# Swin attention and a Fourier layer on one core: the division of the first sixteen rows is split between GpSimd and ScalarE, and the mode scalings change shape and place

## The chip, the cores and the metric

The kernel runs on one core of one Trainium2 chip. The metric is the device time of one execution in microseconds, lower is better. A core has TensorE (PE; its weight loads are listed as PEld), VectorE (DVE), ScalarE (ACT), GpSimd (POOL) and SyncE (SP), which issues nearly all DMAs here. Each engine works through its own list of instructions in order; between engines, semaphores order the work. All data is float32.

## The reference

The input x is 32 images of 56x56 pixels with 128 channels. Two residual layers follow one another, each on a group norm (32 groups of 4 channels, statistics over a whole image).

```python
x = x + L0(_gn(x))     # shifted window attention: 7x7 windows, shift 3, 4 heads of 32 channels
x = x + L1(_gn(x))     # Fourier layer with a feed-forward behind it

# L0, for each window of 49 tokens
qkv  = win @ w_qkv.T                          # q scaled by 32 ** -0.5
attn = softmax(q @ k.T + bias + mask)         # 49 x 49 for each head
out  = (attn @ v) @ w_proj.T + b_proj         # written back unshifted

# L1, once along the width and once along the height
f   = dct(x)[..., :32]                        # 32 modes
g   = einsum(f, w)                            # one 128 x 128 matrix per mode
y   = idct(g, padded with zeros)              # both directions are added
out = relu(y @ W1 + b1) @ W2 + b2             # 512 hidden channels
```

## The kernel before

**Rows and cycles.** An image is cut into 8 rows of 8 windows (NWR = 8), so there are 256 window rows. The program is one loop over cycles, and cycle r starts row r. The stages of a row are spread over cycles: queries, keys, scores, maximum, exponential and v in cycle r (`attn_qk`, `attn_scores`, `attn_max`, `attn_exp`, `attn_v`), the division by the row sums in cycle r+1 (`attn_recip`, `attn_divide`), a transpose in cycle r+2 (`attn_transpose`), the product with v and the projection in cycle r+3 (`attn_values`, `attn_project`), the sums for the second group norm in cycle r+4 (`attn_sums`, `attn_squares`). In between, the input of the next image is turned, its statistics are taken and its first norm is worked out (`norm_step`).

The Fourier layer of image b begins in cycle 8b + 11 (CONV_BEGIN is 11). With c counted from there: c = 0 computes the statistics and the width transform, c = 1 and 2 the two halves of the height transform, c = 3 to 5 mix the modes, c = 5 to 8 transform back, and c = 8, 9, 10, 12, 13, 14, 15 run the seven groups of the feed-forward. These run beside the attention rows of the next two images.

**The order.** The lists of PE, ACT, DVE and POOL are written out by hand: cycles 0 to 10 by `first_rows`, later ones by the calls `halves_first`, `eighths`, `quarters`, `attn_max`, `last_fetch`, `columns_turn`, `behind_max`, `load_first` and `halves_last` of the main loop. Only SyncE's DMAs are placed by a scheduler. Every tile comes from a pool with a tag and a number of buffers (`bufs`); a new tile of a tag waits until the oldest one of the tag has been read for the last time.

**Softmax of a row.** The scores stand in a buffer `a` of 128 partitions x 16 x 49: two windows of 49 rows side by side (partitions 0 to 48 and 64 to 112), 16 groups of 49 columns. VectorE adds bias and mask while it reads PSUM (L486) and takes the maximum (L496), GpSimd subtracts it (L497), ScalarE takes the exponential (L503), VectorE sums (L508) and takes the reciprocal `rs` (L510). Then GpSimd multiplies by `rs` (L522), and at the same time cuts the 49 columns into a block of 32 and one of 17 and moves blocks between groups of 32 partitions, so that one VectorE transpose in blocks of 32x32 (L532) turns all of it. That takes six instructions a row: one of 512 elements and one of 272 on 128 partitions, and two of each on 32 partitions. The result `blocks` has two buffers, taken in turn. There are three buffers `a` for rows 0 to 8 and two later.

**PSUM.** The attention uses four banks in turn (`attn_bank`, tag pa), the rest another four (`conv_bank`, tag pc). A cycle takes a pair for q and k, a pair `po` for the product with v, a pair for the scores, then one for v (`attn_v`) and one for the projection. So v gets the bank that the first of `po` had. Of `po`, u = 0 is read by ScalarE (L579) and u = 1 by VectorE (L577), both into `oT`.

**The statistics and modes.** `fourier_stats` is a generator, and each `next` runs it up to the next `yield`. It averages on TensorE (L650), takes the group sums `ms` (L663), then -mean^2 (L665) and variance + eps (L669) on VectorE, the power -1/2 on GpSimd (L673), and after the first `yield` the shift (L677) on VectorE. The width transform gives four PSUM tiles in c = 0, each half of the height transform two. `turn_modes` transposes each on VectorE into a tile of 448 elements (L715; tag z, four buffers, which also serves the copies of the mixing), and `scale_modes` multiplies it by `rstd` on ScalarE into `y` (L722). There, the 56 lines of one mode lie side by side. `shift_modes` (L727) adds the shift to mode 0. The mixing (L747) reads `y`. In ScalarE's list, the width scalings stand behind v and ahead of exp, the height scalings and both shifts behind exp. `load_columns` (L734, tag htok, two buffers) loads x by columns from DRAM for the height transform: two tiles in c = 0, two in c = 1.

Of the kernel before, what the change touches and what calls it, by code (L numbers as in the profile page):

```python
# [9 lines left out]
F32 = mybir.dt.float32  # L10
AF = mybir.ActivationFunctionType
ALU = mybir.AluOpType
AX = mybir.AxisListType

P = 128
# [32 lines left out]
def swin_fourier_kernel(  # L48
# [33 lines left out]
    def attn_bank():  # L82
        return bank("pa", 4)
# [215 lines left out]
    def attn_buffer(r):  # L299
        return a_sb[r % 3 if r < CONV_BEGIN - 2 else r % 2]  # L300
# [204 lines left out]
    def attn_recip(r):  # L505
# [4 lines left out]
        nc.vector.reciprocal(rs, sm)  # L510
        return rs

    def attn_divide(r, rs):
        a3 = attn_buffer(r).rearrange("p t w j -> p (t w) j")
        dst = blocks[r % 2]
        lo, hi = (slice(0, KB), slice(KB, JP)), (slice(JP, JP + KB), slice(JP + KB, P))
        halves = [(slice(0, P), slice(0, P), k, k) for k in range(2)]
        for a, b in (lo, hi):
            halves += [(a, b, 1, 0), (b, a, 0, 1)]
        for to, src, k, kb in halves:  # L520
            n = (KB, WT - KB)[kb]
            nc.gpsimd.tensor_tensor(  # L522
                dst[to, k, :, :n],
                a3[src, :, kb * KB : kb * KB + n],
                rs[src].unsqueeze(2).to_broadcast([src.stop - src.start, 2 * NWR, n]),
                ALU.mult,
            )
# [7 lines left out]
    def attn_values(im, i, r):  # L535


        v = v_sb[r % 3]
        po = [attn_bank(), attn_bank()]
        HALF = RT // 2  # L540
        po4 = [p[:, :HALF].rearrange("p (r n s) -> p n r s", r=WS, s=WS) for p in po]
        eT = im.eT.pop(i)
# [101 lines left out]
    def fourier_stats(im):  # L644
        pg = attn_bank()

        for k, t in enumerate((im.tot, im.part[:, (NWR - 1) % 4])):
# [13 lines left out]
        )  # L661
        ms = small.tile([P, 2], F32, tag="ms", name="ms")
        nc.vector.tensor_reduce(ms, own, axis=AX.X, op=ALU.add)  # L663
        nm2 = small.tile([P, 1], F32, tag="nm2", name="nm2")
        nc.vector.scalar_tensor_tensor(  # L665
            out=nm2, in0=ms[:, 0:1], scalar=-1.0, in1=ms[:, 0:1], op0=ALU.mult, op1=ALU.mult
        )
        ve = small.tile([P, 1], F32, tag="ve1", name="ve1")
        nc.vector.scalar_tensor_tensor(  # L669
            out=ve, in0=nm2, scalar=1e-5, in1=ms[:, 1:2], op0=ALU.add, op1=ALU.add  # L670
        )
        rstd = small.tile([P, 1], F32, tag="rstd1", name="rstd1")
        nc.gpsimd.tensor_tensor(rstd, ve, mhalf, ALU.pow)  # L673
        im.rstd = rstd
# [33 lines left out]

    def turn_modes(im, width, h):

        im.modes[width, h] = []
        for p in im.py.pop((width, h)):
            t = work.tile([P, 4, C], F32, tag="z", name="modes", bufs=4)
            t = t.rearrange("p k c -> p (k c)")[:, : 2 * CH * KB]
            nc.vector.transpose(t, p[:, : 2 * CH * KB])  # L715
            im.modes[width, h].append(t)

    def scale_modes(im, width, h):

        y = y_of[width][:, : NM * S].rearrange("p (k h n r) -> p h r n k", k=NM, h=2, r=2)[:, h]  # L720
        for r, t in enumerate(im.modes.pop((width, h))):
            nc.scalar.mul(y[:, r], t.rearrange("p (n k) -> p n k", k=NM), im.rstd)  # L722

    def shift_modes(im, width):

# [204 lines left out]
    def divide(cycle):  # L930
        if row(cycle - 1)[0]:
            attn_divide(cycle - 1, attn_recip(cycle - 1))

    def turn(cycle):
        im, i = row(cycle - 2)
        if im:
            attn_transpose(im, i, cycle - 2)
# [54 lines left out]
    def half_columns(cycle, rest=False):  # L992
        for im, c in fourier(cycle):
            if rest and c != 3:
                continue
            if c == 0:
                next(im.stats, None)
            elif c == 3:
                for g in range(2):
                    mix(im, False, g + 2 * rest)  # L1000
            elif c in (4, 5):
                for g in (2 * c - 8, 2 * c - 7):
                    mix(im, True, g)
# [17 lines left out]
    def eighths(cycle):  # L1021
        im, i = row(cycle - 3)
        if im:
            attn_values(im, i, cycle - 3)
        for im, c in fourier(cycle):
            if c == 0:
                for h in range(2):
                    transform(im, True, h)
                    turn_modes(im, True, h)
            if c in (1, 2):  # L1030
                transform(im, False, c - 1)
                if c == 1:
                    for g in range(2):
                        load_columns(im, g + 2)
# [10 lines left out]

    def first_scale(cycle):
        for im, c in fourier(cycle):
            if c == 0:
                shift_modes(im, True)
            elif c in (1, 2):  # L1050
                scale_modes(im, False, c - 1)
                if c == 2:
                    shift_modes(im, False)

    def width_scale(cycle):
        for im, c in fourier(cycle):
# [43 lines left out]
    def halves_last(cycle):  # L1100
        im, i = row(cycle)
        if im:
            attn_v(im, i, cycle)
        width_scale(cycle)
        if has_ff(cycle):
            half_columns(cycle)
        half_columns(cycle, True)
# [3 lines left out]
            norm_step(cycle)  # L1111
        if row(cycle)[0]:
            attn_exp(cycle)
        first_scale(cycle)
        im, j = row(cycle - 3)
        if im:
            last_out(cycle)
# [11 lines left out]
    def first_rows(cycle):  # L1129
# [23 lines left out]
        next_tokens(cycle)  # L1153
        if im:
            attn_v(im, i, cycle)
        if cycle == 0:
            for half in range(2):
                bias_and_mask(nc.vector, 1, 1, half)
# [20 lines left out]
    with tc.manual_schedule(engines={ET.PE, ET.Activation, ET.DVE, ET.Pool}):  # L1179
# [15 lines left out]
        for cycle in range(NB * NWR + CONV_BEGIN + FF_AT[-1] - NWR + 1):  # L1195
# [4 lines left out]
            if not row(cycle - 3)[0]:  # L1200
# [4 lines left out]
                half_columns(cycle)  # L1205
                half_columns(cycle, True)
                first_scale(cycle)
                load_first(cycle)
                last_out(cycle)
                quarters(cycle)  # L1210
# [76 lines left out]
```

## Time and profile before

| | us |
|---|---|
| three runs: median (lowest to highest) | 3299.6 (3297.3 to 3299.78) |
| the profiled execution | 3297.98 |
| its span, first to last instruction | 3296.2 |

| engine | busy us | share of the span | instructions |
|---|---|---|---|
| PE | 3170.4 | 96% | 65408 |
| PEld | 2394.9 | 73% | 65408 |
| DVE | 2605.2 | 79% | 5098 |
| ACT | 2057.4 | 62% | 3680 |
| POOL | 2335.7 | 71% | 2610 |

| line, engine, what | count | mean ns |
|---|---|---|
| L497 POOL subtract the maximum, 128x784 | 253 | 1508 |
| L522 POOL divide, 128x512 / 128x272 | 253 / 253 | 1061 / 660 |
| L522 POOL divide, 32x512 / 32x272 | 506 / 506 | 1054 / 655 |
| L503 ACT exp, 128x784 | 253 | 859 |
| L722 ACT scale modes, 128x448 | 256 | 1122 |
| L715 DVE transpose modes, 128x448 | 256 | 619 |
| L755 ACT copy of the mixing, 128x512 | 256 | 589 |
| L809 ACT copy xf, 128x448 | 192 | 594 |
| L351 ACT copy of wrapped rows, 128x168 | 31 | 337 |
| L629 ACT square, 128x512 / 128x384 | 128 / 128 | 719 / 617 |
| L532 DVE transpose of blocks, 128x1024 | 256 | 1225 |

The profile is one execution, recorded by the hardware; L numbers are lines of the kernel before. Three kinds of its answers are used below. A timeline line gives start and duration in us, engine, line, operation, tile written and tiles read, shapes and count, and in brackets how long the engine had been idle and what released it; a few instructions of one group are merged into one line, with the time from the first start to the last end. A line of waits gives the waiting instruction, its releaser, the total in us, the number of times, and the longest. In a table by stage, each row is one stretch of the run with the busy time of each engine and the number of instructions, then the granted TensorE clock, the share of DMA time and GB/s. Because engine times overlap, shares say little about what a saving is worth: that depends on which wait ends last at the place in question.

### The profile page before, as it was taken

Reading aid. Unit: us, or ns where it says so; the run is one execution under the profiler, and the core shown is the slowest. Engines: PE = TensorE matmul, PEld = TensorE weight load, DVE = VectorE, ACT = ScalarE, POOL = GpSimd, SP = SyncE. Lnnn points to the kernel's source line nnn. Section 1 sums busy time; section 2 is a strip of 40 time slices with the busy share of each in tenths; the row PEclk is TensorE's granted clock in tenths of the full one; section 3 lists DMA queues with packets and bytes.
Section 4 is the critical chain, followed back from the end, with each engine's and each line's share of the span. In section 5 each row is a group of like instructions: output and inputs, shape, how many; then the busy total and the mean of one; then the engine's idle time right before and its main releaser. Section 6 shows DMA issues by size and latency. Waiting matters only on the chain.

```text
span 3296.2 us, 151336 instructions
## 1 busy us (share of the span) xinstructions
PE 3170.4 (96%) x65408; PEld 2394.9 (73%) x65408; DVE 2605.2 (79%) x5098; ACT 2057.4 (62%) x3680; POOL 2335.7 (71%) x2610
## 2 busy tenths in 40 slices
PE   4689999999999999999999999999999999999999
PEld 3467777777777777777777777777777777777776
DVE  7888888887888878888888888877888887888751
ACT  3456666666666666666666666666666666666663
POOL 7777777777777777777777777777777777777741
PEclk9799999999999999999999999999999999999999
DMA  6555555555555555555555555555555655555453
GB/s 105 116 124 142 140 138 142 133 146 140 137 140 135 136 145 138 138 142 138 139 144 143 136 142 138 136 142 143 137 139 136 143 139 139 138 143 135 121 140 96
DMA packets 1168160, 448.40 MB, mean 136 GB/s; under 512 B 520107, under 2 KB 1137629, under 8 KB 1167493
## 3 DMA queue, kind: packets, MB, share of 16 engines
q1 hardware_dynamic: 1159300, 437.38, 54.9%
q8 instruction: 514, 8.42, 1.1%
q10 hardware_dynamic: 7584, 1.18, 0.3%
q14 instruction: 154, 1.25, 0.1%
q0 software_dynamic: 608, 0.17, 0.0%
HBM read 276.97 MB, written 161.48 MB: 133 GB/s over the span
## 4 chain that ended last, share of the span: by engine, by line
PE 76%; ACT 10%; DVE 7%; POOL 3%; DMA 2%; issue 2%; SPq 1%; ACTq 0%; POOLq 0%; DVEq 0%
PE pc L113 35%; PE pa L113 9%; PE pa L456 7%; PE pc L747 5%; PE pc L786 5%; PE pa L592 5%; PE pa L478 4%; PE pa L547 4%; ACT k L443 2%; PE pc L699 2%; ACT hid L830 2%; ACT y L722 2%; POOL a L497 2%; DVE modes L715 1%; DVE a L486 1%
## 5 line engine op out<-in xcount | busy, mean ns | idle before, releaser
L522 POOL TENSOR_TENSOR blocks<-a,rs 128x512 f32<-128x512 f32 x1518 | 1289.4, 856 | 483.9 <-DVE rs L510 263.0
L113 PE MATMUL pc<-wff,hid 128*64 128x128 f32 x12544 | 742.0, 273 | 1.3 <-ACT hid L830 1.0
L113 PE MATMUL pc<-xf,wff 128*64 128x512 f32 (+2 forms) x3584 | 718.9, 539 | 1.1 <-DVE xf L804 0.9
L113 PEld LDWEIGHTS pc<-wff,hid 128*64 128x64 f32 x12544 | 706.5, 137 | 11.1 <-ACT hid L830 5.3
L497 POOL TENSOR_TENSOR a<-a,mx 128x784 f32<-128x784 f32 x253 | 381.4, 1508 | 314.9 <-DVE mx L496 281.6
L113 PEld LDWEIGHTS pc<-xf,wff 128*64 128x64 f32 x3584 | 280.6, 136 | 354.9 <-issue 239.9
L830 ACT ACTIVATE hid<-pc,b1sb 128x512 f32<-128x512 f32 (+2 forms) x896 | 499.4, 643 | 42.7 <-PE pc L113 42.7
L463 ACT COPY v<-pa 128x512 f32<-128x512 f32 x256 | 151.9, 593 | 482.8 <-PE pa L456 482.7
L113 PE MATMUL pa<-xw,wn 128*64 128x392 f32 x2048 | 400.4, 501 | 31.3 <-ACT wn L412 28.8
L865 DVE TENSOR_TENSOR res<-pc,res 128x512 f32<-128x512 f32 (+3 forms) x257 | 142.9, 567 | 319.4 <-issue 173.2
L503 ACT ACTIVATE a<-a 128x784 f32<-128x784 f32 x253 | 217.3, 859 | 281.4 <-POOL a L497 281.4
L486 DVE TENSOR_TENSOR a<-pa,bm 128x392 f32<-128x392 f32 x506 | 261.1, 557 | 84.8 <-PE pa L478 70.6
L837 POOL TENSOR_TENSOR res<-res,b2sb 128x512 f32<-128x512 f32 (+2 forms) x256 | 265.3, 1042 | 87.4 <-DMA res<-scr 78.4
L443 ACT ACTIVATE k<-pa,bqkv,heads 128x392 f32<-128x392 f32 x512 | 318.1, 673 | 8.0 <-PE pa L113 0.9
L532 DVE STREAM_TRANSPOSE eT<-blocks 128x1024 f32<-128x1024 f32 x256 | 313.6, 1225 | 2.4 <-POOL blocks L522 2.4
L127 POOL TENSOR_TENSOR xr<-xr,bproj 128x384 f32<-128x384 f32 (+1 forms) x256 | 292.8, 1144 | 25.6 <-DMA xr<-in_x_dram 17.1
L456 PE MATMUL pa<-wn,xw 128*64 128x128 f32 x4096 | 289.5, 283 | 8.6 <-issue 2.5
L547 PEld LDWEIGHTS pa<-eT,v 49*32 49x32 f32 x16384 | 173.6, 106 | 154.3 <-ACT hid L830 48.7
L592 PE MATMUL pa<-wproj,oT 128*64 128x128 f32 x3584 | 251.8, 276 | 19.6 <-DVE oT L577 17.4
L508 DVE TENSOR_REDUCE sm<-a 128x16 f32<-128x784 f32 x253 | 243.0, 961 | 23.9 <-ACT a L503 23.8
L456 PEld LDWEIGHTS pa<-wn,xw 128*64 128x64 f32 x4096 | 225.5, 139 | 48.5 <-ACT oT L579 16.9
L722 ACT ACTIVATE y<-modes,rstd 128x448 f32<-128x448 f32 x256 | 252.0, 1122 | 4.4 <-DVE modes L715 4.4
(110 smaller groups left out, 4908.3 us busy)
## 6 DMA issues: line engine op xcount, KB each, us to landing
zscr<-z SPq DMA_DIRECT2D x512, 112.0 KB
xin<-in_x_dram SPq DMA_DIRECT2D x496, 112.0 KB
htok<-scr SPq DMA_DIRECT2D x256, 196.0 KB
zT<-zscr SPq DMA_DIRECT2D x192, 256.0 KB
res<-scr SPq DMA_DIRECT2D x160, 256.0 KB
out_dram<-res SPq DMA_DIRECT2D x160, 256.0 KB
scr<-x SPq DMA_DIRECT2D x256, 112.0 KB
xr<-in_x_dram SPq DMA_DIRECT2D x256, 84.0 KB
```

Source lines behind the costliest of these rows:

```text
L113: nc.tensor.matmul(dst[ps], lhsT=lhsT[:, ps], rhs=rhs, start=start, stop=stop)
L127: nc.gpsimd.tensor_tensor(piece, piece, bproj.unsqueeze(1).to_broadcast([P, n, C]), ALU.add)
L443: nc.scalar.activation(k_sb[:, u], pk[:, :RT].rearrange("p (w j) -> p w j", j=WT), AF.Identity, bias=im.bias[:, 3 + u : 4 + u], scale=head ...
L456: nc.tensor.matmul(pv[HALVES[w % 2], w // 2 * C : (w // 2 + 1) * C], lhsT=im.half[i // NP][:, t0 : t0 + JP], rhs=im.w[:, 2 * C : 3 * C], s ...
L486: nc.vector.tensor_tensor(a[:, 2 * hp : 2 * hp + 2, :, 0:WT].rearrange("p u w j -> p w u j"), ps[hp][:, :RT].rearrange("p (w u j) -> p w u ...
L497: nc.gpsimd.tensor_tensor(a3, a3, mx.unsqueeze(2).to_broadcast([P, 2 * NWR, WT]), ALU.subtract)
L522: nc.gpsimd.tensor_tensor(dst[to, k, :, :n], a3[src, :, kb * KB : kb * KB + n], rs[src].unsqueeze(2).to_broadcast([src.stop - src.start, 2 ...
L532: nc.vector.transpose(eT.rearrange("p t (k j) -> p k t j", k=2), blocks[r % 2])
L547: nc.tensor.matmul(po4[u][h * HD : (h + 1) * HD, pr], lhsT=v[ks, pr, h * HD : (h + 1) * HD], rhs=eT[ks, h * NP + pr, :WT], start=True, sto ...
L592: nc.tensor.matmul(pp[hs, (n - n0) * C : (n - n0 + 1) * C], lhsT=oT[:, t0 : t0 + JP], rhs=wproj, start=True, stop=True,)
L722: nc.scalar.mul(y[:, r], t.rearrange("p (n k) -> p n k", k=NM), im.rstd)
L830: nc.scalar.activation(hf[:, :n], ph[:, :n], AF.Relu, bias=b1sb[:, f : f + 1])
```

## The change

- `attn_divide`: for rows 0 to 15 (r < CROSS_END = 16), GpSimd multiplies the whole buffer `a` by `rs` in place, in one instruction of 128x784. The cutting and moving into `blocks` is then done by six ScalarE copies, `attn_cross`. They stand at the end of `first_rows`, behind v, in cycles up to 10, and behind exp in cycles 11 to 16. From row 16 on the division is as before.
- `attn_values`: the two banks of `po` are swapped between u = 0 and u = 1.
- `fourier_stats`: a `yield` behind the group sums; what follows runs between the transposes of the two halves of the width modes. The variance takes one VectorE instruction (mean^2 - mean of squares) and one on GpSimd (times -1, plus eps).
- `turn_modes` and `scale_modes`: for the width and for the second half of the height, both transposes of a half go into one tile of 896 elements, of tag htok, and one ScalarE instruction scales it. It reads at a step of 32 elements and writes runs of 28. The first half of the height keeps two tiles and two instructions of 448, now in another order of elements.
- In ScalarE's list, the height scalings and the height shift now stand behind the width scalings, ahead of exp (`first_scale`); the width shift stays behind exp (`width_shift`).

```diff
+    CROSS_END = CONV_BEGIN + 5
+
+    def attn_cross(r):
+        a3 = attn_buffer(r).rearrange("p t w j -> p (t w) j")
+        dst = blocks[r % 2]
+        lo, hi = (slice(0, KB), slice(KB, JP)), (slice(JP, JP + KB), slice(JP + KB, P))
+        halves = [(slice(0, P), slice(0, P), k, k) for k in range(2)]
+        for a, b in (lo, hi):
+            halves += [(a, b, 1, 0), (b, a, 0, 1)]
+        for to, src, k, kb in halves:
+            n = (KB, WT - KB)[kb]
+            nc.scalar.copy(dst[to, k, :, :n], a3[src, :, kb * KB : kb * KB + n])
+
     def attn_divide(r, rs):
         a3 = attn_buffer(r).rearrange("p t w j -> p (t w) j")
+        if r < CROSS_END:
+            nc.gpsimd.tensor_tensor(
+                a3, a3, rs.unsqueeze(2).to_broadcast([P, 2 * NWR, WT]), ALU.mult
+            )
+            return
...
-        po = [attn_bank(), attn_bank()]
+        po = [attn_bank(), attn_bank()][::-1]
...
         nc.vector.tensor_reduce(ms, own, axis=AX.X, op=ALU.add)
-        nm2 = small.tile([P, 1], F32, tag="nm2", name="nm2")
+        yield
+        nvar = small.tile([P, 1], F32, tag="nm2", name="nm2")
         nc.vector.scalar_tensor_tensor(
-            out=nm2, in0=ms[:, 0:1], scalar=-1.0, in1=ms[:, 0:1], op0=ALU.mult, op1=ALU.mult
+            out=nvar,
+            in0=ms[:, 0:1],
+            scalar=ms[:, 0:1],
+            in1=ms[:, 1:2],
+            op0=ALU.mult,
+            op1=ALU.subtract,
         )
         ve = small.tile([P, 1], F32, tag="ve1", name="ve1")
-        nc.vector.scalar_tensor_tensor(
-            out=ve, in0=nm2, scalar=1e-5, in1=ms[:, 1:2], op0=ALU.add, op1=ALU.add
-        )
+        nc.gpsimd.tensor_scalar(ve, nvar, -1.0, 1e-5, ALU.mult, ALU.add)
...
     def turn_modes(im, width, h):
+        py = im.py.pop((width, h))
+        if width or h:
+            t = work.tile([P, CH, C], F32, tag="htok", name="modes", bufs=2)
+            t = t.rearrange("p n c -> p (n c)")
+            dst = t.rearrange("p (n r k) -> p r n k", r=2, k=NM)
+            for r in range(2):
+                nc.vector.transpose(dst[:, r], py[r][:, : 2 * CH * KB])
+            im.modes[width, h] = [t.rearrange("p (s k) -> p k s", k=NM)]
+            return
         im.modes[width, h] = []
-        for p in im.py.pop((width, h)):
+        for p in py:
...
-            im.modes[width, h].append(t)
+            im.modes[width, h].append(t.rearrange("p (n k) -> p k n", k=NM))

     def scale_modes(im, width, h):
-        y = y_of[width][:, : NM * S].rearrange("p (k h n r) -> p h r n k", k=NM, h=2, r=2)[:, h]
-        for r, t in enumerate(im.modes.pop((width, h))):
-            nc.scalar.mul(y[:, r], t.rearrange("p (n k) -> p n k", k=NM), im.rstd)
+        y = y_of[width][:, : NM * S].rearrange("p (k h s) -> p h k s", k=NM, h=2)[:, h]
+        modes = im.modes.pop((width, h))
+        for r, t in enumerate(modes):
+            nc.scalar.mul(y[:, :, r :: len(modes)], t, im.rstd)
...
+    def cross(cycle):
+        if 0 < cycle <= CROSS_END:
+            attn_cross(cycle - 1)
...
@@ half_columns @@
-            if c == 0:
-                next(im.stats, None)
-            elif c == 3:
+            if c == 3:
...
@@ eighths @@
                     transform(im, True, h)
                     turn_modes(im, True, h)
+                    if h == 0:
+                        next(im.stats)
...
@@ first_scale @@
-            if c == 0:
-                shift_modes(im, True)
-            elif c in (1, 2):
+            if c in (1, 2):
...
+    def width_shift(cycle):
+        for im, c in fourier(cycle):
+            if c == 0:
+                shift_modes(im, True)
...
@@ halves_last @@
         width_scale(cycle)
+        first_scale(cycle)
...
             attn_exp(cycle)
-        first_scale(cycle)
+        cross(cycle)
+        width_shift(cycle)
...
@@ first_rows @@
             attn_v(im, i, cycle)
+        cross(cycle)
```

More of the change, by code (lines that the diff above doesn't have):

```diff
@@ L1207, in swin_fourier_kernel @@
                 first_scale(cycle)
+                width_shift(cycle)
                 load_first(cycle)
```

## The prediction

> **What bounds the kernel now.** I read the page's busy shares and its 40 slices first, then busy time by stage, then who waited for whom in the full stretch, then the timelines of the start and of one image late in the run.
>
> ```profile
> PE   4689999999999999999999999999999999999999
> ...
> PEclk9799999999999999999999999999999999999999
> ```
> ```profile
> 0.00:100.00 100.00, 51.53 (x1006) 36.98 (x1006) 81.62 (x187) 38.03 (x68) 72.16 (x108) 0.91 0.60 102
> 100.00:200.00 100.00, 69.99 (x1474) 51.71 (x1478) 76.34 (x151) 48.23 (x84) 73.31 (x84) 0.78 0.56 125
> 200.00:300.00 100.00, 92.32 (x1907) 66.90 (x1900) 82.14 (x160) 62.50 (x112) 72.31 (x79) 1.00 0.55 131
> 300.00:400.00 100.00, 99.22 (x2134) 75.10 (x2123) 82.57 (x162) 65.30 (x119) 73.68 (x83) 1.00 0.57 140
> ```
> The columns after the length are busy PE, PEld, DVE, ACT, POOL, then the clock granted to TensorE. From 300 us on TensorE is busy 99% of the time: it is the bound, and another engine saves something there only by removing a TensorE wait. The first 300 us are different: TensorE idles 48.5 + 30.0 + 7.7 = 86 us of them. There a chain through all engines sets the pace.
>
> ```profile
> PE pc L747 <- ACT y L727: 14.8, 29, 1.7
> PE pc L786 <- issue: 6.5, 11, 1.1
> ```
> This is the list of TensorE's waits from 290 to 3190 us (total, times, longest). Busy time there is 2866.7 of 2900, so 33 us are idle, and the largest item is the mode mixing waiting for ScalarE's shift of y: 14.8 us in 29 images, about 0.5 us each.
>
> In the start, one cycle looks like this (timeline, cycle 3 to 4, GpSimd alone):
> ```profile
> 53.98 1.51 POOL L497 TENSOR_TENSOR a<-a,mx 128x784 f32<-128x784 f32 x1
> 55.44 5.35 POOL L522 TENSOR_TENSOR blocks<-y,rs 128x512 f32<-128x512 f32 x6
> ...
> 61.02 1.27 POOL L127 TENSOR_TENSOR xr<-xr,bproj 128x512 f32<-128x512 f32 x1
> 62.24 1.50 POOL L497 TENSOR_TENSOR a<-a,mx 128x784 f32<-128x784 f32 x1
> ```
> GpSimd has no gap: 1.50 + 5.35 + 1.27 + 0.10 = 8.2 us, the cycle. The change attacks this. But row 1's subtract starts at 39.11 and row 10's at 121.09: 9.1 us a cycle on average, since VectorE and loads hold some cycles. The other chain, seen where GpSimd doesn't hold (cycle 1):
> ```profile
> 34.75 1.25 ACT L443 ACTIVATE k<-pa,bqkv,heads 128x392 f32<-128x392 f32 x2
> ...
> 36.05 0.91 PE L478 MATMUL pa<-k,q 64*64 64x98 f32 x32 [1.41 <-ACT k L443]
> ...
> 36.99 1.04 DVE L486 TENSOR_TENSOR a<-pa,bm 128x392 f32<-128x392 f32 x2 [1.26 <-PE pa L478]
> ...
> 38.06 0.97 DVE L496 TENSOR_REDUCE mx<-a 128x16 f32<-128x784 f32 x1
> ...
> 39.11 1.50 POOL L497 TENSOR_TENSOR a<-a,mx 128x784 f32<-128x784 f32 x1 [4.63 <-DVE mx L496]
> ```
> Keep this chain in mind: k, scores, add, max, subtract follow each other with hops below 0.1 us.
>
> **What the Trainium skill says.** "ScalarE: Activation LUTs", section "What ACT_TABLE_LOAD costs": an ACTIVATE takes 186 ns + 0.833 ns per element, 93 ns more for each pointer operand, and neighbours overlap by about 93 ns. The trace agrees for copies: 128x168 in 337 ns (326 by the law), 128x512 in 589 (613). "Vector Engine (DVE) Microarchitecture Reference", section "5.2 Measured stream behaviour on trn2 (trn3 not measured)": full rate needs pairs of adjacent words; single words with hops between cost more on whichever side hops. It measured VectorE, but ScalarE's trace agrees: the mode scaling, which writes single words 56 apart, takes 1122 ns for 448 elements (652 by the law), while the xf copy, which writes pairs, takes 594. "TensorE: Matmul & The Clock Gate", section "What's actually happening": after an idle window of some 3.4 us the clock is halved. The trace has the scores at 0.91 us or at 1.58.
>
> **Part 1: the in-place divide and ScalarE's copies, rows 0 to 15.** Removed: six GpSimd products a row, 5.35 us. Added: one product of 128x784, by the subtract's row (same shape, in place) 1.50 us, and six ScalarE copies. Their cost: 3 x 0.589 + 3 x 0.414 (272 elements, between the 168 and 512 rows) = 3.01, less 0.11 overlap each (two z copies of 589 take 1.07 together): 2.4 us. Bounds: 2.2 to 3.1, the upper end if they cost what Square from SBUF does (719 for 512). ScalarE idles 7 to 14 of each 20 us there, so its busy share isn't the issue; its order is. In the first 11 cycles the instruction order on ScalarE is q, k, exp, oT, square, v, the six copies of row r-1, then q and k of row r+1. The copies wait for the product of row r-1, which stands on GpSimd behind the subtract of row r, which waits for row r's maximum, scores, and k. So a new ring closes: k end, scores 0.91 (1.58 at half clock), add 1.04, max 0.97, subtract 1.50, product 1.50, copies 2.4, q and k back to back 1.7, hops 0.15: 10.2 us, or 10.8 at half clock. TensorE now idles some 4 us just ahead of the scores (values can run about 5.4 us after k, when eT is there), so half clock there is likely part of the time: I take 10.5. VectorE's own work in the heaviest cycles (two quarter turns with bn_stats: 58.12 to 69.48 less 1.8 of waiting, 9.6) stays below. So 9 x (10.5 - 9.1) = +12.5, and 1 for the wrap copy and the bias operations, now in the ring: row 10's subtract comes some 13.5 us late.
>
> Cycle 11 gives back: before, TensorE waited 5.06 us for tot behind a 5.34 us divide, and VectorE 4.30 for rstd behind the next; both shrink with the product and the later variance. Row 11's subtract is then about +9, but exp now stands behind the width scalings and the copies follow exp ahead of q: +12 at k of row 12. In cycles 12 to 16 the ring is max (3.2 after k), then in 12 and 13 modes 1.1 and scaling 2.0, exp 0.8, copies 2.4, q and k 1.7: 11.2. Together with 9.9, 12.5 (norm chain, less waiting than before) and 11.5 that is 56.5, against 56.6 from k of row 12 (144.3) to k of row 17 (200.9). The mix wait of 4.05 in cycle 14 is in this. Start in all: +11 us, bounds +3 (full clock, cheap scalings) and +20 (copies at 3.1). Behind row 16 TensorE fills up, and the delay stays to the end.
>
> **Part 2: scalings and their place.** Width and second height half: one instruction of 896 elements instead of two of 448. Writes become runs, but reads now hop by 32 words. Below: 186 + 93 + 746 = 1.0 us, if reads hop free; above: 2.4, if they hop worse than writes do now (1.05 ns extra). I take 2.0, what the pair takes now (2.02): no saving. The first height half hops on both sides: 2.0 to 2.8 a pair. What matters is the place. One image now:
> ```profile
> 2041.19 2.02 ACT L722 ACTIVATE y<-modes,rstd 128x448 f32<-128x448 f32 x2
> 2043.24 0.34 ACT L727 ACTIVATE y<-y,shift 128x56 f32<-128x56 f32 x1
> ```
> Modes were ready at 2039.87; scaling moves ahead of exp (start 2040.43), so y is done at about 2042.2 instead of 2043.58, and the mixing, free to start at 2043.1, waits no longer: -14.8 us over the full stretch. Exp ends at about 2043.0, and its reader on VectorE starts at 2043.32: covered, 0.3 us to spare; beyond that VectorE is late by the excess, with about 1 us idle behind it.
>
> **Part 3: the modes tile moves from the pool of z to that of htok.** Those buffers (two) are also where the height columns land. Now they are loaded at 2006.83 (four issues, 1.83 us) and first used by TensorE at 2021.76. After the change they wait on SyncE's queue for the two width scalings: v ends at 2012.86, so free at 2014.8 and 2016.8, last issue 2018.6, 3.2 us before use (the second half is read 0.5 later). Now the queue emptied 4.3 us after the last issue, but with some 0.7 MB of other traffic; from 2013 to 2018 it was nearly idle. I take no stall; bounds 0 and 1 us an image. Behind the waiting issue stand the out store and scr writes of that cycle (2016.98 now), late by under 2 us and needed much later; the res load of the next group moves from 2019.41 to about 2031, ahead of its bias add near 2040.
>
> **Part 4: the swapped banks and the variance.** The v matmuls then wait for VectorE's oT instead of ScalarE's. Weight loads waited 16.1 us in 55 cases, the matmuls under 0.15 us each; VectorE is ahead in one of two cycles (2047.10 against 2047.24): -1 us, bounds 0 and -4. One tiny VectorE operation less and one GpSimd operation more per image, off TensorE's path: nothing.
>
> **Sum.** +11 - 14.8 - 1 = -5 us. The profiled execution took 3297.98 (span 3296.2 and 1.8 around it), which gives 3293; the median shown is 3299.6, 1.6 above it. I forecast 3294.
>
> **Rivals.** (a) The start loses nothing: TensorE keeps full clock, the scalings become cheap, and loads that stalled cycles 7 to 10 are hidden. For: the 8.2 us GpSimd cycle is gone and 3.8 us load waits are visible. Against: the ring of 10.2. Start -2: 3281. (b) The ring is dearer: copies 3.1 and half clock throughout, 11.5 a cycle: start +26, 3309. For: the clock of 0.72 to 0.88 between 60 and 200 us. Against: copies of 337 and 589 fit the law. (c) Slower by the htok buffers: if the columns land later than about 3.7 us after the last issue, TensorE's height transform stalls in each image; at 0.8 us late, 31 images, +26: 3320. It decides as soon as scalings of 896 take more than about 2.4 us. (d) "Denser" saves no time, as taken above; if it does, (a) gains, (c) falls.
>
> **Chances.** Forecast 0.55 (own range 3285 to 3303: 0.22 faster, 0.29 same, 0.04 slower), (a) 0.18 (nearly all faster), (b) 0.13 (mostly slower), (c) 0.14 (slower). Faster by over 0.2% (6.6 us, about what a measurement of this kernel can tell from no change) 0.39, within 0.34, slower 0.27. Range: 3280, which leaves out half of (a), to 3310, which leaves out most of (c).
>
> **What would show it.** Copies of blocks on ScalarE near 2.4 us a row; subtracts of rows 1 to 10 spaced 10 to 11 us, with ScalarE's first copy waiting for GpSimd; the mixing's wait on y gone from TensorE's list; scalings of 896 near 2 us; no wait of TensorE on htok loads. Spacing below 9 us, or a new TensorE wait at the height transform, would prove me wrong.

## The result and the profile after

The changed kernel is slower: 3326.35 us (median of four runs, 3325.34 to 3326.98) against 3298.45 us for the kernel before in the same comparison, a ratio of 1.0087 with a 95% interval of 1.0074 to 1.0100. The profiled execution has a span of 3324.3 us (before: 3296.2). The forecast was 3294, between 3280 and 3310, so it missed by 32 us.

Two views of the changed kernel answer to those shown of before: its 40 slices, and busy time in stretches of 100 us (columns as before: length, busy PE, PEld, DVE, ACT, POOL, then the granted clock).

```profile
PE   3679999999999999999999999999999999999999
...
PEclk8779999999999999999999999999999999999999
```
```profile
0.00:100.00 100.00, 45.57 (x724) 33.37 (x724) 64.58 (x150) 41.58 (x76) 40.93 (x63) 0.85 0.54 88
100.00:200.00 100.00, 64.64 (x1246) 47.84 (x1246) 71.16 (x145) 67.83 (x122) 37.04 (x41) 0.76 0.49 104
200.00:300.00 100.00, 87.18 (x1800) 63.34 (x1798) 79.83 (x155) 66.26 (x117) 62.30 (x68) 0.91 0.49 120
300.00:400.00 100.00, 98.98 (x2052) 74.29 (x2050) 82.01 (x160) 65.60 (x115) 73.13 (x82) 1.00 0.58 142
```

TensorE does less in each of the first three stretches, and so does VectorE. GpSimd's busy time in the first 200 us fell from 145.5 to 78 us, and nothing became faster by it, for another chain now sets the pace of the start. ScalarE's rose by 23 us.

I split the span at one mark, the start of k of row 17 (first line before, second after):

```profile
199.66 1.24 ACT L443 ACTIVATE k<-pa,bqkv,heads 128x392 f32<-128x392 f32 x2
```
```profile
231.22 1.24 ACT L443 ACTIVATE k<-pa,bqkv,heads 128x392 f32<-128x392 f32 x2
```

Before, 3096.5 us follow; after, 3093.1. **So the start lost 31.6 us, and the rest gained only 3.4**, which is no more than the rest varies between kernels that should not differ there (see the table below). The prediction had +11 and -15.8.

**The start.** A ring is a closed chain: each step waits for the one before it, and the last one sets off the first again. This is one turn of it in the changed kernel (timeline, instructions of the ring alone):

```profile
42.14 3.15 ACT L524 COPY blocks<-a 128x512 f32<-128x512 f32 x6 [3.49 <-POOL a L529]
...
45.30 0.59 ACT L433 ACTIVATE q<-pa,bqkv 128x392 f32<-128x392 f32 x1
45.79 1.24 ACT L443 ACTIVATE k<-pa,bqkv,heads 128x392 f32<-128x392 f32 x2
...
47.08 1.59 PE L478 MATMUL pa<-k,q 64*64 64x98 f32 x32 [7.74 <-ACT k L443]
...
48.70 1.04 DVE L486 TENSOR_TENSOR y<-pa,bm 128x392 f32<-128x392 f32 x2 [6.71 <-PE pa L478]
49.77 0.97 DVE L496 TENSOR_REDUCE mx<-y 128x16 f32<-128x784 f32 x1
...
50.82 1.50 POOL L497 TENSOR_TENSOR y<-y,mx 128x784 f32<-128x784 f32 x1 [8.71 <-DVE mx L496]
...
52.28 1.50 POOL L529 TENSOR_TENSOR a<-a,rs 128x784 f32<-128x784 f32 x1
...
53.82 0.97 ACT L524 COPY blocks<-a 128x512 f32<-128x512 f32 x2 [2.61 <-POOL w1sb L264]
```

Each line starts where the one above ends, and the last is the first again, 11.68 us later (a timeline cut at its window shows only two of the six copies there). The brackets say how long each engine had idled: TensorE 7.74 us, VectorE 6.71, GpSimd 8.71, ScalarE 3.49. No engine is busy all the time; the ring is closed. (The 2.61 put down to w1sb is the product's: the memset stands between it and the next GpSimd work.) Subtracts of rows 1 to 10 are 11.8 us apart (39.15 to 145.53, nine cycles), before 9.1.

**The rest.** TensorE's waits in the full stretch, 320 to 3220 us, of the changed kernel (total, times, longest):

```profile
PE pa L456 <- ACT oT L597: 23.1, 36, 0.8
```

The mixing's wait on y, 14.8 us before, is gone, as forecast. In its place, the v matmul (L456) waits for oT, about 0.75 us in each of 28 images, in the cycle with c = 4; the eight other waits are of 0.15 to 0.18 us. Traced back in the changed kernel:

```profile
2072.52 5.35 POOL L540 TENSOR_TENSOR blocks<-a,rs 128x512 f32<-128x512 f32 x6 [1.53 <-DVE rs L510]
...
2077.95 1.51 POOL L497 TENSOR_TENSOR a<-a,mx 128x784 f32<-128x784 f32 x1
...
2079.49 0.86 ACT L503 ACTIVATE a<-a 128x784 f32<-128x784 f32 x1 [1.55 <-POOL a L497]
...
2084.56 0.66 DVE L595 TENSOR_SCALAR oT<-pa,bqkv 128x147 f32<-128x147 f32 x3
2084.74 0.47 ACT L597 ACTIVATE oT<-pa,bqkv 128x196 f32<-128x196 f32 x1
...
2085.27 1.10 PE L456 MATMUL pa<-wn,xw 128*64 128x128 f32 x16 [0.75 <-ACT oT L597]
```

The maximum of this row ended at 2076.38, but its subtract stands behind the six products of the row before, to 2077.95. Exp waits for it; VectorE's sums, and a norm's small operations behind them, wait for exp; VectorE's oT stands behind those, and v needs the bank that oT frees. (The list names ScalarE's oT. It hangs on the same exp, behind which ScalarE has no gap, and both oT copies end within 0.01 us of each other, at 2085.21 and 2085.22.) The products in turn began when the row before was summed. From its add (2064.52) to v it is 20.75 us. In the kernel before, the same stations stand at the same distances:

```profile
2044.71 5.34 POOL L522 TENSOR_TENSOR blocks<-a,rs 128x512 f32<-128x512 f32 x6 [1.54 <-ACT k L443]
...
2050.14 1.50 POOL L497 TENSOR_TENSOR a<-a,mx 128x784 f32<-128x784 f32 x1
...
2051.67 0.86 ACT L503 ACTIVATE a<-a 128x784 f32<-128x784 f32 x1 [0.91 <-POOL a L497]
...
2056.73 0.66 DVE L577 TENSOR_SCALAR oT<-pa,bqkv 128x147 f32<-128x147 f32 x3
2056.92 0.47 ACT L579 ACTIVATE oT<-pa,bqkv 128x196 f32<-128x196 f32 x1
...
2057.44 1.09 PE L456 MATMUL pa<-wn,xw 128*64 128x128 f32 x16
```

(The bracket of the products names k; `rs` ended at 2044.56, 0.15 us ahead of them, as far ahead as in the changed kernel.) There it is 20.73 us from the add (2036.71) to v, and both oT copies end at 2057.39, 0.05 us ahead of v. TensorE's list of waits doesn't show this, for TensorE had already lost its time at the mixing; but the slack was nothing.

### The profile page after: what moved, and what is told of

It reads as the page before. It is cut to its first block, busy times and chain, and to the rows that moved or that the text cites. A ratio compares the mean times of both kernels' runs of the same rounds, so it can differ in the third digit from the quotient of the medians.

```text
span 3324.3 us, 151132 instructions
## 1 busy us (share of the span) xinstructions
PE 3177.1 (96%) x65408; PEld 2404.8 (72%) x65408; DVE 2593.3 (78%) x5066; ACT 2114.2 (64%) x3680; POOL 2285.7 (69%) x2562
## 4 chain that ended last, share of the span: by engine, by line
PE 77%; ACT 12%; DVE 5%; POOL 2%; issue 2%; DMA 1%; SPq 1%; ACTq 0%; POOLq 0%; DVEq 0%
PE pc L113 36%; PE pa L113 8%; PE pa L456 7%; PE pc L818 5%; PE pa L478 5%; PE pa L610 4%; PE pc L779 4%; PE pa L565 4%; PE pc L721 3%; ACT k L443 2%; ACT hid L862 2%; DVE modes L739 2%; ACT y L754 2%; ACT blocks L524 1%; ACT xr L647 1%
## 5 line engine op out<-in xcount | busy, mean ns | idle before, releaser
L540 POOL TENSOR_TENSOR blocks<-a,rs 32x272 f32<-32x272 f32 (+3 forms) x1440 | 1223.8, 857 | 471.4 <-DVE rs L510 302.2
L456 PE MATMUL pa<-wn,xw 128*64 128x128 f32 x4096 | 293.7, 286 | 30.6 <-ACT oT L597 26.1
L754 ACT ACTIVATE y<-modes,rstd 128x896 f32<-128x896 f32 (+1 forms) x160 | 249.7, 1601 | 83.7 <-DVE modes L739 48.6
L478 PE MATMUL pa<-k,q 64*64 64x98 f32 x8192 | 240.2, 255 | 55.3 <-ACT k L443 55.3
L456 PEld LDWEIGHTS pa<-wn,xw 128*64 128x64 f32 x4096 | 229.8, 141 | 70.2 <-ACT oT L597 40.8
```

Of the source, the lines that this page charges most:

```text
L456: nc.tensor.matmul(pv[HALVES[w % 2], w // 2 * C : (w // 2 + 1) * C], lhsT=im.half[i // NP][:, t0 : t0 + JP], rhs=im.w[:, 2 * C : 3 * C], s ...
L478: nc.tensor.matmul(ps[hp][HALVES[e], pr * 2 * WT : (pr + 1) * 2 * WT], lhsT=q[cs, w * WT : w * WT + JP], rhs=k_sb[cs, :, w], start=True, s ...
L540: nc.gpsimd.tensor_tensor(dst[to, k, :, :n], a3[src, :, kb * KB : kb * KB + n], rs[src].unsqueeze(2).to_broadcast([src.stop - src.start, 2 ...
L754: nc.scalar.mul(y[:, :, r :: len(modes)], t, im.rstd)
```

## The experiments

My theory A: the start's loss is the ring through the copies, and the steady gain is hidden because two chains of equal length, one through the scalings and one through the division, meet in each image. All runs first; each ratio is to the runs of the kernel before in the same comparison (medians 3296.35 to 3298.45), and "rest" is the profiled span less the start of k of row 17.

| kernel | us | ratio to before (95%) | subtract of row 10 | k of row 17 | rest |
|---|---|---|---|---|---|
| before | 3298.45 | | 121.09 | 199.66 | 3096.5 |
| changed | 3326.35 | 1.0087 (1.0074 to 1.0100) | 145.53 | 231.22 | 3093.1 |
| e1 no copies | 3297.53 | 1.0001 (0.9992 to 1.0009) | 122.14 | 198.96 | 3094.5 |
| e2 copies alone | 3330.99 | 1.0098 (1.0084 to 1.0112) | 145.52 | 234.41 | 3094.1 |
| e3 no copies, no bank swap | 3299.18 | 1.0001 (0.9993 to 1.0009) | 122.03 | 199.91 | 3098.6 |
| e4 no copies, late division | 3321.24 | 1.0069 (1.0056 to 1.0082) | 121.93 | 200.79 | 3117.2 |
| e5 product ahead of scores | 3314.00 | 1.0053 (1.0039 to 1.0066) | 130.18 | 218.76 | 3094.0 |
| e6 no copies, split division | 3274.48 | 0.9931 (0.9917 to 0.9944) | 121.65 | 200.12 | 3072.6 |
| e7 e5's order and e6's split | 3279.79 | 0.9948 (0.9936 to 0.9961) | 129.95 | 205.84 | 3073.9 |
| e8 two of six copies | 3300.11 | 1.0008 (1.0000 to 1.0017) | 126.78 | 199.90 | 3095.2 |
| e9 before, split division | 3292.72 | 0.9990 (0.9982 to 0.9998) | 120.85 | 200.00 | 3092.5 |
| e10 copies to row 9 | 3319.70 | 1.0074 (1.0061 to 1.0088) | 145.55 | 223.62 | 3093.7 |
| e11 copies a cycle later | 3279.70 | 0.9946 (0.9932 to 0.9959) | 126.64 | 205.42 | 3071.6 |

Nothing done to the start moves the rest: it lies between 3092.5 and 3098.6 in every kernel with the division in its old place in the cycles c = 3, and in e9. So a difference of 3 us in the rest of single profiles means nothing.

### Which part costs: e1 and e2

e1 is the changed kernel with

```diff
-    CROSS_END = CONV_BEGIN + 5
+    CROSS_END = 0
```

> The changed kernel with the division of all rows as before (six GpSimd products, no ScalarE copies); the mode scalings, the later variance and the swapped banks stay. Theory A (the whole loss comes from the start, through the ring k, scores, add, max, subtract, product, six copies, next q and k): subtracts of rows 1 to 10 about 9.1 us apart again, k of row 17 within 5 us of the kernel before, and in all 3296, between 3290 and 3301, ratio to the kernel before 0.999. Theory B (a good part of the loss is in the scalings, their place in ScalarE's list or the buffers of the modes): above 3312, ratio above 1.004.

e2 puts `attn_cross`, the in-place product and the two calls of `cross` into the kernel before, and nothing else.

> The kernel before with one part of the change alone: product in place and six ScalarE copies for the first sixteen rows. Theory A: subtracts of rows 1 to 10 spaced 11.8 us, k of row 17 some 30 us later than in the kernel before, in all 3329, between 3324 and 3334, ratio 1.009. Theory B (the copies cost little alone, and only together with the scalings ahead of exp in cycles 11 to 16 do they cost 30): 3310 to 3320, with k of row 17 late by 12 to 20.

Measured: without the copies 3297.53, as before; with them alone 3330.99. Both confirm A, and rival B is out: the whole loss is the copies and the product in place. Beside the copies, the other edits even helped the start a little: in these two profiles k of row 17 is 3.2 us earlier in the changed kernel than in e2. And e1 shows the other half: scalings, later variance and swapped banks together change nothing that can be measured. Its largest wait in the full stretch:

```profile
PE pa L456 <- ACT oT L597: 23.3, 40, 0.8
```

### Is it the copies' time: e8

The changed kernel, with the four copies on 32 partitions left out:

```diff
-        for to, src, k, kb in halves:
+        for to, src, k, kb in halves[:2]:
             n = (KB, WT - KB)[kb]
             nc.scalar.copy(dst[to, k, :, :n], a3[src, :, kb * KB : kb * KB + n])
```

> The changed kernel with only the two ScalarE copies on 128 partitions; the four on 32 partitions, which move blocks between groups of partitions, are left out, so a part of the exponentials isn't moved. They take 0.63 + 0.43 us twice, 2.1 us of 3.15. Theory A (the copies stand in the ring, microsecond for microsecond): subtracts of rows 1 to 10 spaced 9.7 us in place of 11.8, row 10's subtract near 126 us; in all 3301, between 3294 and 3308, ratio 1.001. Rival F (the ring is set by something else than the copies' time, such as TensorE's half clock or their waiting): spacing stays above 11, time above 3315.

Measured: 3300.11, spacing 9.8 us (38.50 to 126.78), row 10's subtract at 126.78, all as A expected. One cycle of it:

```profile
60.44 0.97 ACT L524 COPY blocks<-y 128x512 f32<-128x512 f32 x2 [2.38 <-POOL w1sb L264]
...
69.77 0.97 ACT L524 COPY blocks<-a 128x512 f32<-128x512 f32 x2 [1.64 <-POOL w1sb L264]
```

The copies fell by 3.15 - 0.97 = 2.18 us, the spacing by 2.0. So in rows 1 to 10 the copies' time goes into the cycle nearly one for one, and rival F is out. Over the whole start, 31.3 us for 2.18 us a row are 14.4 rows' worth, of 16. Row 10's subtract is still 5.7 us later than in the kernel before, but k of row 17 is level with it (199.90 against 199.66).

### Can the ring be opened: e5, e11, and where it costs: e10

e5 is the changed kernel with the product moved out of the ring, in `first_rows` alone:

```diff
+        divide(cycle)
         if im:
             attn_scores(im, i, cycle)
             attn_max(cycle)
-        divide(cycle)
         turn(cycle)
```

> The changed kernel with one edit: in rows 1 to 10 the sums, reciprocal and in-place product of a row stand ahead of the scores, maximum and subtract of the next one, on VectorE and GpSimd alike; the six ScalarE copies stay where they are. Theory A (the product behind the subtract closes the ring; without this link the copies can run while TensorE and VectorE work out scores and maximum): subtracts of rows 1 to 10 between 8.5 and 9.7 us apart in place of 11.8, row 10's subtract between 118 and 130 us in place of 145.5, and 3303, between 3298 and 3310, ratio to the kernel before 1.0015; what stays is the loss of rows 11 to 16. Rival E (the copies cost their time on ScalarE wherever they stand, since ScalarE itself is the limit of the start): spacing above 11, time above 3318.

Measured: spacing 10.1 us, row 10's subtract at 130.18, 3314.00. All three miss what A expected, though the link counts for 1.7 us a cycle; rival E's bounds (above 11 us, above 3318) aren't reached either. Rows 11 to 16, where the edit doesn't reach, add another 10 us (row 10's subtract is 9.1 late, k of row 17 is 19.1 late). In the profile of e5 the copies no longer wait for the product, which ends at 66.47, but for v:

```profile
62.67 0.86 ACT L503 ACTIVATE a<-a 128x784 f32<-128x784 f32 x1
...
63.42 0.44 ACT L597 ACTIVATE oT<-pa,bqkv 128x196 f32<-128x196 f32 x1
...
63.92 1.98 PE L610 MATMUL pa<-wproj,oT 128*64 128x128 f32 x16
...
65.68 1.65 PE L456 MATMUL pa<-wn,xw 128*64 128x128 f32 x16
...
67.38 0.59 ACT L463 COPY v<-pa 128x512 f32<-128x512 f32 x1 [3.03 <-PE pa L456]
...
67.86 3.16 ACT L524 COPY blocks<-a 128x512 f32<-128x512 f32 x6
...
71.03 0.59 ACT L433 ACTIVATE q<-pa,bqkv 128x392 f32<-128x392 f32 x1
```

k, exp, oT, projection, v, copies, q: another ring through the same copies, 9.97 us from q (61.06) to q. The projection (L610) waits for oT, which stands behind exp on ScalarE, and v stands behind the projection on TensorE. e11 therefore goes back to the changed kernel and moves the copies away from q, one cycle later and behind exp, for rows 0 to 8 (with the division split as in e6 below, so it compares with e6):

```diff
         if cycle:
             attn_exp(cycle - 1)
+        cross(cycle)
...
             attn_v(im, i, cycle)
-        cross(cycle)
```

> As the kernel with product and copies for the first rows, the scalings and the split division, but the product stands behind the scores and subtract again, only rows 0 to 8 are divided in this way, and the six copies of a row stand one cycle later, behind k and the exponential, so that q and k of the next row no longer wait for them. Theory A (the copies cost because q and k stand behind them; without the copies the ring k, scores, add, max, subtract, product is no longer closed): subtracts of rows 1 to 9 spaced 8.3 to 9.4 us, the start not later than in the kernel before, and as with the split division alone or better: 3273, between 3266 and 3279, ratio 0.993. Rival E (the copies cost about 3 us of ScalarE a cycle wherever they stand, through oT and v behind them): spacing 10 or more and 3280 or more.

Measured: 3279.70 against 3274.48 of e6; k of row 17 is 5.8 us later than in the kernel before. The subtracts are 9.8 us apart in the mean, and 10.8 from row 3 to row 10 (51.23 to 126.64), where each cycle has copies. A's forecast fell. Rival E's bounds (10 us, 3280) are just missed in the mean, but the wait that it named is there: oT stands behind the copies, and TensorE waits for oT ahead of the projection:

```profile
69.75 3.14 ACT L524 COPY blocks<-a 128x512 f32<-128x512 f32 x6
...
72.92 0.44 ACT L597 ACTIVATE oT<-pa,bqkv 128x196 f32<-128x196 f32 x1
...
73.42 1.06 PE L610 MATMUL pa<-wproj,oT 128*64 128x128 f32 x12 [3.35 <-ACT oT L597]
```

So opening one link was not enough in either trial: ScalarE feeds TensorE at three points of each of these cycles (q and k, oT, v), and both places tried put the 3 us ahead of one of them. Other places weren't tried.

e10 ends the copies at row 9 (`CROSS_END = CONV_BEGIN - 1`).

> The changed kernel with the product in place and the copies for the first ten rows alone; rows 10 to 15 are divided as before. Theory A (rows 10 to 15 carry a loss of their own, since there ScalarE has the width scalings as well, and the ring is still closed): row 10's subtract late by 24 as in the changed kernel, the k of row 17 late by about 19 in place of 31.6, in all 3315, between 3310 and 3320, ratio 1.005. Rival H (the loss is made in rows 1 to 10 and is only carried on): within 4 us of the changed kernel, 3322 to 3330.

Measured: 3319.70, k of row 17 at 223.62, so 24.0 late, in place of 31.6. The time is within A's bounds, the mark 5 us later than expected. So most of the loss is made in rows 1 to 10, as rival H had it, but its 3322 at least is not reached: the copies of rows 10 to 15 carry some 7 us of their own by the marks (31.6 less 24.0), 4 to 7 by the times.

### Where the steady gain went: e3, e4, e6, e9

e3 is e1 with the banks in their old order (`[::-1]` removed).

> As the kernel with the division of all rows as before, and the two banks of the product with v not swapped. Theory A (the v matmul of c = 4 waits because both oT copies come late, at the end of the chain through VectorE and GpSimd): the wait of v on an oT copy is still there, about 0.75 us in each image, and the time is within 2 us of the same kernel with swapped banks. Theory C (the swap made the wait, since ScalarE's oT is now the one that v waits for): the wait is gone from the list and the time is 10 to 20 us lower.

Measured: 3299.18, the same ratio as e1, and the wait of v on oT is there with the same 23.3 us. The swap is nothing, since both oT copies end together; theory C is out.

e4, from e1, puts the six products of cycles with c = 3 behind the subtract.

> As the kernel with the division of all rows as before, and in cycles with c = 3 GpSimd's six products of the division stand behind the subtract of the next row, not ahead of it. Theory A (the gain of the earlier scalings is hidden by a chain of 20.7 us: scores of c = 2, VectorE, division, subtract behind it, exp, sums, oT, v of c = 4): subtract, exp and oT of c = 3 come up to 5 us earlier, the wait of v on oT is gone, the 14 us come out: 3283, between 3278 and 3289, ratio to the kernel before 0.995. Theory D (some other chain, for example the later division and transpose, is as long as this one): a new wait of TensorE of 0.5 us or more per image in another place, and the time within 4 us of the kernel with the division ahead.

Measured: 3321.24, 24 us slower than e1. A was right that the wait of v would go (1.4 us are left), and wrong on what follows. Rival D was right that a new wait would come, but it expected the time of e1. TensorE's waits in e4, and the place in its timeline:

```profile
PE pa L113 <- ACT wn L412: 36.7, 28, 1.3
...
PE pa L456 <- ACT oT L597: 1.4, 9, 0.2
```
```profile
2061.93 1.50 POOL L497 TENSOR_TENSOR a<-a,mx 128x784 f32<-128x784 f32 x1 [5.48 <-DVE mx L496]
...
2063.39 5.36 POOL L540 TENSOR_TENSOR blocks<-a,rs 128x512 f32<-128x512 f32 x6
...
2070.06 5.37 POOL L540 TENSOR_TENSOR blocks<-a,rs 128x512 f32<-128x512 f32 x6
...
2075.50 1.50 POOL L497 TENSOR_TENSOR a<-a,mx 128x784 f32<-128x784 f32 x1
...
2076.96 0.55 POOL L404 TENSOR_TENSOR rstd<-ve,mhalf 128x1 f32<-128x1 f32 x1
...
2078.22 0.88 PE L113 MATMUL pa<-xw,wn 128*64 128x392 f32 x4 [1.33 <-ACT wn L412]
```

GpSimd idles 5.48 us ahead of the subtract that the products now follow, and this was time it needed: two small operations, the next row's division, its subtract and the power for the next image's norm follow without a gap and come late. ScalarE scales the weights `wn` of the next image by that power, and TensorE waits for them, 1.33 us here. So e6 moves only half of them, since the chain is just 0.75 us too long:

```diff
             rs = attn_recip(cycle - 1)
-            attn_divide(cycle - 1, rs)
+            if any(c == 3 for _, c in fourier(cycle)) and row(cycle)[0]:
+                late[cycle] = rs
+                attn_divide(cycle - 1, rs, slice(0, 3))
+            else:
+                attn_divide(cycle - 1, rs)
...
                 attn_max(cycle)
+                late_divide(cycle)
```

`attn_divide` takes the part of its six products as an argument, and `late_divide` issues the last three.

> The division of all rows as before and no copies, and in cycles with c = 3 three of GpSimd's six products of the division stand ahead of the subtract of the next row and three behind it. Theory A (the chain through the division hides the gain; it is 0.75 us too long in each image, and putting 2.6 us of it behind the subtract takes it off, while the next division, and with it the power for the next image's norm, comes in time since GpSimd was idle ahead of the subtract): waits of v on oT gone and no new one above 0.2 us an image; 3277, between 3271 and 3285, ratio to the kernel before 0.994. Theory D (behind the division there is always another chain as long): a new wait of 0.5 us or more an image, 3292 or more.

Measured: 3274.48, ratio 0.9931 (0.9917 to 0.9944), 23 us better than e1 and the best of all. Its waits:

```profile
PE pc L818 <- issue: 6.3, 9, 1.0
...
PE pa L456 <- ACT oT L597: 0.6, 4, 0.2
```

The remaining corner is the split without the scalings: e9 makes e6's edit in the kernel before.

> The kernel before with one edit alone: in cycles with c = 3 three of GpSimd's six products of the division stand ahead of the subtract of the next row and three behind it. Theory A (two chains of nearly the same length end in the same stretch of each image, the scalings and shift ahead of the mixing, and the division ahead of oT and v; taking either away alone gives nothing): the mixing's wait on y stays near 14.8 us, 3296, between 3289 and 3301, ratio 0.9995. Rival G (the division's chain alone sets the pace of an image, and the moved scalings are worth nothing): about as fast as with both, 3276, ratio 0.994.

Measured: 3292.72, ratio 0.9990 (0.9982 to 0.9998), within A's bounds. The mixing still waits:

```profile
PE pc L747 <- ACT y L727: 13.2, 29, 0.5
```

The four corners: neither edit 1, the scalings' edits alone 1.0001, the split alone 0.9990, both 0.9931. By the medians the first alone is worth nothing, the second alone 3 to 4 us, both together 23. That is what two chains of one length do, and rival G is out.

e7 joins e5's order (copies to row 9) with the split.

> Product in place and copies for the first ten rows alone, with the product ahead of the scores; the division of later rows as before, and split around the subtract in cycles with c = 3. If both mechanisms hold as told: start no later than in the kernel before, by up to 5 us earlier, no wait of v on oT: 3276, between 3268 and 3285, ratio 0.993. If the copies cost their time anyway: above 3295.

Measured: 3279.79, within its bounds, but its start is 6.2 us later than the kernel before's, and it is 5 us slower than e6: the copies have nothing to offer in this form either.

## Why the prediction was wrong

**The bound and the two places** (the ring at the start, the mixing's wait in each later image) were right, and so was "ScalarE's order is the issue, not its busy share". Two terms failed. The start was taken at +11 us and lost 31.6: its mechanism was right, its size wrong. The gain behind it was taken at 15.8 us and came to 3.4: its mechanism was incomplete. So some 20 of the 32 us of the miss lie in the start and some 12 in the rest.

**Part 1, the cycle of 10.5 us.** Measured 11.8. Of the sum's terms, add, maximum, subtract, product, q and k held (1.04, 0.97, 1.50, 1.50, 1.73). Two were mis-sized. The copies were taken at 2.4 us and took 3.15, above the upper bound of 3.1. The mean durations are 0.63 us for 512 elements and 0.43 for 272, close to the 0.589 and 0.414 assumed (+0.17 in all); the overlap of 0.11 at each hand-off is what failed. "ScalarE: Activation LUTs", section "What ACT_TABLE_LOAD costs", says that neighbours overlap by about 93 ns. Here the first two, on 128 partitions, do, by 0.09; those on 32 partitions don't (timeline of the changed kernel, two short windows):

```profile
42.14 0.97 ACT L524 COPY blocks<-a 128x512 f32<-128x512 f32 x2 [3.49 <-POOL a L529]
```
```profile
43.14 1.07 ACT L524 COPY blocks<-a 32x512 f32<-32x512 f32 x2
```

0.63 + 0.43 = 1.06: the first pair is shorter than that, the second not. The other term was the scores: taken between 0.91 and 1.58 (10.5 us is the mean of the two cases), they took 1.59 in this cycle, at a granted clock of 0.50, and 1.58 to 1.69 in eight of the nine cycles of rows 2 to 10. These two make 0.75 + 0.35 of the 1.3 us. Over nine cycles that is row 10's subtract at +24.4 in place of +13.5.

**Part 1, cycle 11** gave back 3.8 us of the 24.4 by row 11's subtract, close to the 4.5 forecast, but k of row 12 was late by 24.7 again (forecast 12). **Cycles 12 to 16** failed: the sum said 56.5 against 56.6 us; it was 63.4 (167.78 to 231.22). The copies are a term of this sum too, and e10, without them there, took 57.7 (165.95 to 223.62). Their extra 0.75 us in five cycles is 3.8 of the 6.9 us; where the rest lies was not traced.

**Part 2, the scalings' cost** was right: 1.92 us for 896 elements against 2.0 taken, two of 448 at 1.12 each as before, so "denser" saves next to nothing. The wait on y went, as forecast. **The step that failed is to count this wait, 14.8 us, as a gain.** The prediction asked whether exp's readers were covered, but not what is late next on TensorE: in the same image, v started 0.05 us after both oT copies, and in the changed kernel it waits 23.1 us in all for oT. Removing either chain alone left the time nearly where it was (e1 1.0001, e9 0.9990); with both gone the gain is there (e6).

**Part 3** held: no wait on htok in the full stretch. Four such waits, 3.4 us in all, lie outside it, nearly all of that in the start. **Part 4**: the swap was taken at -1 and is nothing (e3 against e1).

**The rivals.** (b), copies at 3.1 and half clock throughout, described the start: +26 for 31.6. Its 3309 fell short because it kept the steady gain; less that gain it would have said 3324. (c) didn't happen. What no case contained was that the start's loss and the missing gain could come together. The prediction's signs of being wrong, a spacing below 9 us or a new wait at the height transform, did not show: the new wait came at v, where no sign had been set.

## What to carry to other kernels

Before you count a wait of the bounding engine as a gain, list the hand-offs to it in the same period that have next to no slack. They don't show in its list of waits, and one of them can keep the time unless it is shortened too, as oT's did here. Shorten a chain by about what it is too long (here three products of six moved behind one subtract) and not by much more (all six moved cost 24 us). Work taken off one engine and put on another can cost its full time if it stands in a ring that sets the pace, as the copies did in rows 1 to 10: draw the ring ahead of the change and after it. And price TensorE's link in it at the slow end where TensorE idles for some 4 us in each turn, as here.

## What the runs showed of the hardware that I had not expected

- ScalarE copies that move blocks on 32 partitions took as long as those on 128 (0.629 us against 0.626 for 512 elements, 0.431 against 0.430 for 272), and didn't overlap with their neighbours, while a pair on 128 partitions overlapped by 0.09 us. Whether the partitions or the order in one destination tile decide was not tried.
- The slow scores are those at a low granted clock, and the idle time just ahead of them doesn't tell alone which they are. In the changed kernel, with 4.1 to 7.7 us of idle time ahead, eight of the nine scores of rows 2 to 10 took 1.58 to 1.69 us at a clock of 0.50, one 1.16 at 0.72. In e8, scores with 2.29 us of idle time ahead took 1.49 at 0.55, others with 2.09 took 0.90 at 1.00. In e5 they took 0.91 at 1.00 with 3.41 us ahead, and 1.53 at 0.53 with 2.29.
- Behind k of row 17, e6 takes 23.9 us less than the kernel before, but TensorE's idle time there fell only from 47.4 to 31.4 us. The other 8 us are in its busy time (3049.2 and 3041.2 us), though the matmuls are the same in number and shape. The largest single difference is in the matmuls of the height mixing (L747 before, L779 in e6, reading w1sb: 126.0 and 122.7 us over the whole span). Why these records are shorter was not tested.
